# Layer 0 of a four-layer graph network: block sums made by accumulating transfers, the second half of x loaded early, its statistics on ScalarE

## The chip, the cores and the metric

The kernel runs on one core of one Trainium2 chip. The metric is the device time of one execution in microseconds; before the change the median of three executions is 2145.6 us (2143.03 to 2153.62). Five engines work side by side, each through its own list of instructions in order: TensorE (PE, with its weight loads PEld), VectorE (DVE), ScalarE (ACT), GpSimd (POOL) and SyncE (SP). SP and POOL issue the transfers, each through a queue of its own (q1 is SP's, q0 is POOL's), and 16 DMA engines carry them out. An instruction that waits holds back all that stand behind it on its engine.

## The reference, cut to what matters

x has 2708 rows and 512 columns, adj is 2708 by 2708, all in f32. Four layers follow each other; all have the product of a scaled adjacency matrix with a normalized x, and layer 0 is

```python
h = jnp.maximum(_layernorm(x, axis=-1), 0.0)
deg = jnp.sum(adj, axis=1)
dinv = (deg + 1.0) ** (-0.5)
aug = dinv[:, None] * (adj + jnp.eye(n)) * dinv[None, :]
x = x + jax.nn.relu(aug @ h @ weight)
```

## The kernel before

**Tiling.** The rows of x stand as 22 tiles of 128 rows by 512: 20 full ones (`NF`), five to each of four quarters, and two that hold what is left of the quarters (`NF`, `NF + 1`). The transposed adjacency stands in HBM as blocks `yb[j, i, u]` of 128 x 5 x 339 numbers (847.5 KB; j and i are quarters, u one of two halves of the 677 columns), and rows for the two odd tiles (`yt`).

**The products.** adj times h is done with Winograd's seven products on two levels. The outer seven, called p1 to p7 here, are in `OUTER`: p1 takes `XA` (tiles 0 to 9, first 256 columns) and y11 as it is, p2 `XC` and y21, p3 `XC` and y22, p4 `XD` and t4, p5 `XB` and t1, p6 `XA` and t2, p7 `XA` and t3. XB has the second 256 columns of tiles 0 to 9, XC and XD those of tiles 10 to 19. Their sums are t1 = y12 + y11, t3 = y22 + y12, t2 = y22 + t1 = t3 + y11 and t4 = t2 + y21, each of 2 x 2 blocks (`QUAD`, written (0,0), (0,1), (1,0), (1,1)) and two halves u; `keep_o` stores them through POOL's queue for the later layers (`osum`). `add_loops` puts the identity of aug into diagonal blocks. X itself is rewritten in place between the products (`by_halves`: XA - XB before p7; XA = -XD - XA before p6).

One `multiply` is one outer product for one u. It makes seven inner products of five matmuls each (L475; the trace counts each f32 matmul twice, so x10), in the order 1, 6, 2, 7, 5, 4, 3. `inner_x` (L436 to L439) forms s1 to s4 of the X side, `inner_y` (L449 to L452) forms t1, t2, t4 and t3 of the four blocks o11, o12, o21, o22. ACT copies product 1 into v (L503), DVE makes u2 and u3 (L507, L513), and `give` (L492, L494, L487) brings the results into `agg`. Product 6 needs inner t2, product 7 inner t3, product 4 inner t4.

**The order of layer 0** (`first_aggregate`). All first loads are for the degrees: PE adds up the blocks' columns (L275), `quarter_columns` and `first_h` turn the sums into dinv and write relu of the normalized x with it into h (L221). So h's first half is ready after the blocks of two quarters. Then follow, with u = 0 and 1 each, p1 and p7; beside p7 the degrees of the other half (`other_degrees`), and after it `first_h` for tiles 10 to 21; then p6, p2, p4 for u = 1, the same for u = 0; the odd tiles' products of quarters 0 and 1 (`tails`, L526, L531, L566); p5 for u = 0 and 1; the other tails, `epilogue`, p3, `epilogue`.

**Sums in layer 0.** `third_sums` (L644) forms t3 on DVE from y22 in its place and y12 in a spare block; `second_sums` (L651) adds t3 to y11 for t2, for both u; `first_stats` (L202, L203) takes mean and variance of x's second half on DVE, after its load (L238, L240) behind p7's first half. `first_sums` forms t1 by a load of y12 (L402) and a transfer that adds y11 to what lies in SBUF (`accum_op`, L697, issued by POOL), block by block; `add_loops` on its diagonal blocks (L410) and the stores follow one product later. Three spare blocks lie in the second half of h (`spare`), three in `agg` (`early`), three in `ends` (`more`).

**What sets the order.** The instructions are put in each engine's list when the program is built, by a scheduler. `tc.issue_after(i)` holds what is under it until after instruction i; the lists `at_u2`, `at_u3`, `at_end` and `at_t4` collect such instructions. Nothing reorders the lists on the chip. Transfers of SP use eight semaphores in turn, so that each waits for the landing of the one eight places before it.

Of the kernel before, what the change touches and what calls it, by code (L numbers as in the profile page):

```python
# [12 lines left out]
P = 128  # L13
# [24 lines left out]
def gnn_kernel(  # L38
# [178 lines left out]
        )  # L217
        return b

    def normalized(t, src, scale, shift):  # L220
        nc.scalar.activation(h[:, t, :], src, AF.Relu, bias=shift, scale=scale)  # L221

    def groups(ts):

# [17 lines left out]
    def first_stats(ts):  # L242
        for t in ts:
            stats(h[:, t, :], mv0[:, t, :])

# [68 lines left out]
    def other_degrees(u, ys):  # L314

        if u == 0:
            parts[1, 1] = upool.tile([P, W], FP, tag="s", name="row")
        for b, blocks in ((0, (ys[1], ys[2])), (1, (ys[7],))):
            ps = ps_out.tile([P, W], FP, tag="out", name="dg_ps")
            tl = tail_place(b, u)  # L320
            column_sums(ps, [tl[:, 0], tl[:, 1]], blocks, parts[b, u])
        if u < U - 1:
            return
# [15 lines left out]
    def first_h(columns, looped):  # L339

        ts = list(columns)
        n, t0 = len(ts), ts[0]
        span = slice(t0, t0 + n)
        pd = ps_sm.tile([P, NT], FP, tag="sm", name="pd")
        for s, t in enumerate(ts):
            nc.tensor.matmul(
                pd[:, s : s + 1], columns[t], ones[:, 0:1], start=True, stop=True
            )
        if looped:
            nc.vector.tensor_copy(deg[:, t0 : t0 + looped], pd[:, :looped])  # L350
        if looped < n:
            nc.vector.tensor_scalar(
                deg[:, t0 + looped : t0 + n], pd[:, looped:n], 1.0, None, ALU.add
            )
        rsqrt(dinv[:, span], deg[:, span], n)
        mv = mv0[:, span, :]
        rstd = rstd_of(mv, n)
        nc.vector.tensor_mul(rstd[:, :n], rstd[:, :n], dinv[:, span])
        sh = shift_of(mv, rstd, n)
        for s, t in enumerate(ts):  # L360
            normalized(t, h[:, t, :], rstd[:, s : s + 1], sh[:, s : s + 1])

    def other_roots():

# [55 lines left out]
        nc.vector.scalar_tensor_tensor(o, a, -1.0, b, ALU.mult, ALU.subtract)  # L420

    at_u2, at_u3, at_end, at_t4 = [], [], [], []

    def inner_x(X):
        n = half // 2
# [14 lines left out]
    def inner_y(blks, u, loops, t3=None):  # L442
# [8 lines left out]
        at_t4.append(nc.vector.tensor_add(t4, o21, t2).ins)  # L451
        nc.vector.tensor_add(t3, o22, o12)  # L452
        return {1: o11, 2: o21, 3: o22, 4: t4, 5: t1, 6: t2, 7: t3}

# [9 lines left out]
            multiply(xs_, inner_y(blks, u, loops), u, dests)  # L464
            free.extend(blks)

    def multiply(xs_, ys, u, dests):


        cu = slice(u * W, (u + 1) * W)  # L470
# [12 lines left out]
        def give(a, b, ps, part, op):  # L483
# [5 lines left out]
            for fh, ih, how in dests:  # L489
                d = agg[:, fh, ih, a, b, cu]  # L490
                if part is not None:
                    at_end.append(nc.vector.tensor_tensor(d, ps, part, op).ins)  # L492
                elif how == "added":
                    nc.vector.tensor_add(d, d, ps)  # L494
                elif how == "less":
                    nc.vector.tensor_sub(d, ps, d)
# [6 lines left out]
        nc.scalar.copy(v, pa)  # L503
        pb = bank("pb")
        product(pb, 6, True)
        u2 = upool.tile([P, W], FP, tag="u2", name="u2", bufs=2)
        at_u2.append(nc.vector.tensor_add(u2, v, pb).ins)  # L507
        product(pa, 2, False)
        give(0, 0, pa, None, None)
        pc = bank("pc")  # L510
        product(pc, 7, True)
        u3 = upool.tile([P, W], FP, tag="u3", name="u3")
# [38 lines left out]
    def tails(self_loops, qs, loaded=None):  # L551

        for q in qs:
            blk, both = loaded[q] if loaded else tail_rows(self_loops, q)
            for u in range(U):
# [7 lines left out]
                tail_products(ps, tl, True)  # L563
                for c in range(NC):
                    d = agg[:, c // 2, q // 2, c % 2, q % 2, u * W : (u + 1) * W]
                    nc.vector.tensor_add(d, d, ps[c])  # L566
            free.append(blk)

    H1 = list(range(0, half))
# [36 lines left out]
    def first_aggregate(epilogue):  # L606
# [25 lines left out]
        t3 = {0: [free.pop(0), free.pop(0), take(early), take(early)], 1: blks[0]}  # L632
        temps = spare + [take(early)]
        p1, p7 = (0, 0, "as it is"), (1, 1, "as it is")
        for u in range(U):
            for b in range(2):
                load_rows(*(tail_place(b, u)[:, s] for s in range(2)), yt[:, :, 2 + b, u])
        xs_ = inner_x(XA)
        multiply(xs_, ys, 0, [p1])
        ys = inner_y(blks[1], 1, 0, own_t3)  # L640

        def third_sums(u):
            for (a, b), blk, y in zip(QUAD, t3[u], temps):
                nc.vector.tensor_add(blk, blk, y)  # L644
                if a == b:
                    add_loops(blk, u, OUTER[7][2])
                keep_o(blk, "t3", a, b, u)

        def second_sums(u):
            for (a, b), t2, y in zip(QUAD, blks[u], t3[u]):  # L650
                nc.vector.tensor_add(t2, t2, y)  # L651
                keep_o(t2, "t2", a, b, u)

        for (a, b), blk, y in zip(QUAD, t3[0], temps):
            load_plain("y22", a, b, 0, blk)
            load_plain("y12", a, b, 0, y)
        with tc.issue_after(at_u2[-1]):
            third_sums(0)
        for (a, b), y in zip(QUAD, temps):
            load_plain("y12", a, b, 1, y)  # L660
        multiply(xs_, ys, 1, [p1])
        second_sums(0)
        by_halves(nc.vector.tensor_sub, XA, XA, XB)
        xs_ = inner_x(XA)
        ys = inner_y(t3[0], 0, 0, own_t3)
        last_sum = at_t4[-1]
        other_degrees(0, ys)
        for (a, b), blk in zip(QUAD, t3[1]):
            load_plain("y22", a, b, 1, blk)
        multiply(xs_, ys, 0, [p7])  # L670
        with tc.issue_after(last_sum):
            third_sums(1)
        first_x(range(half, NT))
        ys = inner_y(t3[1], 1, 0, own_t3)
        with tc.issue_after(at_u3[-1]):
            second_sums(1)
        with tc.issue_after(at_end[-1]):
            first_stats(range(half, NT))
        other_degrees(1, ys)
        multiply(xs_, ys, 1, [p7])  # L680
        first_part_of_both()
        by_halves(minus_sum, XA, XD, XA)
        free += t3[0][:2] + t3[1]

        def among(places):

            for k, f in enumerate(free):
# [1 line left out]
                    return free.pop(k)  # L689
            return free.pop(0)  # L690


        def first_sums(u, places):
            t1 = [among(places) for _ in QUAD]
            for (a, b), blk in zip(QUAD, t1):
                load_plain("y12", a, b, u, blk)
                nc.gpsimd.dma_start(blk, yb[a, b, u], accum_op=ALU.add)  # L697
            with tc.issue_after(at_u3[-1]):
                for (a, b), blk in zip(QUAD, t1):
                    if a == b:  # L700
                        add_loops(blk, u, OUTER[5][2])
                    keep_o(blk, "t1", a, b, u)
            return t1

        for u in reversed(range(U)):
            if u == 1:
                t2 = blks[1]
            else:
                t2 = [among(in_obuf) for _ in QUAD]
                for (a, b), blk in zip(QUAD, t2):  # L710
                    nc.sync.dma_start(blk, osum["t2", a, b, u])
            xs_ = inner_x(XA)
            multiply(xs_, inner_y(t2, u, 0, own_t3), u, [(0, 1, "added")])
            if u == 1:
                other_roots()
                nc.vector.tensor_sub(XB, XB, XD)
            y21 = [among(more) for _ in QUAD]
# [4 lines left out]
            for (a, b), t4, y in zip(QUAD, t2, y21):  # L722
                nc.vector.tensor_add(t4, t4, y)
                keep_o(t4, "t4", a, b, u)
            free += y21
            if u == 0:
                rows = [tail_rows(True, q) for q in (0, 1)]
            xs_ = inner_x(XD)
            multiply(xs_, inner_y(t2, u, 0, own_t3), u, [(1, 0, "as it is")])
            if u == 0:  # L730
                t1 = first_sums(0, more)
            free += t2
# [5 lines left out]
        multiply(xs_, inner_y(t1, 0, 0), 0, p5)  # L738
        free = [f for f in free if all(f is not e for e in more)]
        first = [f for f in t1 if all(f is not e for e in more)]  # L740
        t1 = first_sums(1, in_obuf)
        multiply(xs_, inner_y(t1, 1, 0), 1, p5)
        free += first + t1
        tails(True, (2, 3))
        epilogue(H1)
# [392 lines left out]
```

## Time and profile before

| What | Value |
|---|---|
| Runs, median (lowest to highest) | 2145.6 us (2143.03 to 2153.62) |
| The profiled execution's own time | 2147.35 us |
| Its span | 2145.6 us |
| PE busy | 2068.6 us, 96% |
| DVE busy | 1438.6 us, 67% |
| ACT busy | 384.7 us, 18% |
| Mean traffic | 167 GB/s |

The profile has one row for each instruction with its start, its length, what it writes and reads, and, where the engine was idle before it, how long and what ended the wait. A matmul's end is modelled. Times are counted from the start of the span. Layer 0's products fill the stretch from 35 us to about 449 us; the change touches what runs before 375 us.

### The profile page before, as it was taken

What the parts mean: (1) busy time and instruction counts of PE and PEld (TensorE: products, weight loads), DVE (VectorE), ACT (ScalarE), POOL (GpSimd) and SP (SyncE); (2) the same over time, 40 slices, a digit from 0 to 9 for tenths busy, and PEclk for the clock granted to TensorE, in tenths of its full rate; (3) what the DMA queues carried; (4) which work ended last, traced back from release to release, by engine and by line L of the source; (5) the groups of instructions that cost most, each with busy time, mean ns of one, the idle gap of its engine ahead of it and who ended that gap; (6) DMA issues with size and microseconds to landing.
All of it is one profiled execution on the core that took longest, in us unless ns stands there. A gap on an engine that the chain in (4) does not pass through costs nothing.

```text
span 2145.6 us, 19944 instructions
## 1 busy us (share of the span) xinstructions
PE 2068.6 (96%) x7310; PEld 1289.0 (60%) x7310; DVE 1438.6 (67%) x2513; ACT 384.7 (18%) x755; POOL 173.7 (8%) x319
## 2 busy tenths in 40 slices
PE   5989979999999999999999999999999999999998
PEld 2555646556666645566664546666677666666664
DVE  3888847667666867777576879968537755666512
ACT  1111000222000010100001121000116534444401
POOL 0000010211000020200001130000001000000001
PEclk9999989999999999999999999999999999999999
DMA  9884695446454443644453656544541233233212
GB/s 351 346 336 154 191 281 189 161 153 211 164 177 167 148 165 137 234 164 156 162 183 123 218 196 211 176 156 156 192 166 72 96 101 103 91 101 100 80 41 64
DMA packets 78720, 358.05 MB, mean 167 GB/s; under 512 B 10540, under 2 KB 14508, under 8 KB 78624
## 3 DMA queue, kind: packets, MB, share of 16 engines
q1 hardware_dynamic: 51104, 250.98, 34.3%
q0 software_dynamic: 27520, 105.82, 14.6%
q8 instruction: 57, 0.93, 0.2%
q14 instruction: 39, 0.32, 0.0%
HBM read 294.61 MB, written 62.15 MB: 166 GB/s over the span
## 4 chain that ended last, share of the span: by engine, by line
PE 62%; issue 20%; DMA 8%; DVE 7%; POOL 2%; ACT 1%; SPq 0%; POOLq 0%; DVEq 0%; ACTq 0%
PE pa L475 13%; PE pc L475 12%; PE pd L475 12%; PE po L754 7%; PE pb L475 6%; PE pe L1045 4%; PE pt L526 3%; PE pg L893 3%; DMA obuf<-in_yb_dram 2%; DMA h<-in_x_dram 1%; PE pt L531 1%; DVE ends L846 1%; POOL ends L761 1%; DMA ends<-xs 1%; DMA osumt<-obuf 1%
## 5 line engine op out<-in xcount | busy, mean ns | idle before, releaser
L1045 PE MATMUL pe<-obuf,h 128*128 128x339 f32 x1280 | 372.9, 448 | 0.0
L475 PE MATMUL pa<-obuf,h 128*128 128x339 f32 x1050 | 324.0, 454 | 13.4 <-DVE h L420 8.5
L1045 PEld LDWEIGHTS pe<-obuf,h 128*128 128x128 f32 x1280 | 241.2, 189 | 126.4 <-issue 10.0
L754 PE MATMUL po<-ends,agg 128*128 128x512 f32 x640 | 281.4, 596 | 2.1 <-ACT ends L774 1.9
L475 PEld LDWEIGHTS pa<-obuf,h 128*128 128x128 f32 x1050 | 200.1, 192 | 121.4 <-issue 9.4
L754 PEld LDWEIGHTS po<-ends,agg 128*128 128x128 f32 x640 | 119.8, 190 | 144.8 <-issue 137.3
L475 PE MATMUL pd<-obuf,s 128*128 128x339 f32 x550 | 169.0, 454 | 13.3 <-DVE agg L492 13.3
L475 PE MATMUL pc<-t,h 128*128 128x339 f32 x560 | 173.8, 457 | 4.4 <-DVE u L513 4.4
L966 ACT ACTIVATE e<-r,nsr 128x339 f32<-128x339 f32 x352 | 170.7, 566 | 28.6 <-DVE obuf L970 11.7
L475 PE MATMUL pb<-t,s 128*128 128x339 f32 x560 | 169.3, 448 | 0.1
L475 PE MATMUL pd<-t,s 128*128 128x339 f32 x560 | 169.2, 448 | 0.0
L503 ACT COPY v<-pa 128x339 f32<-128x339 f32 x56 | 24.6, 440 | 758.4 <-PE pa L475 738.8
L475 PEld LDWEIGHTS pd<-obuf,s 128*128 128x128 f32 x550 | 105.6, 192 | 68.0 <-DVE agg L492 14.3
L475 PEld LDWEIGHTS pc<-t,h 128*128 128x128 f32 x560 | 108.1, 194 | 60.9 <-DVE u L513 6.0
L475 PEld LDWEIGHTS pd<-t,s 128*128 128x128 f32 x560 | 106.0, 189 | 54.2 <-issue 0.5
L475 PEld LDWEIGHTS pb<-t,s 128*128 128x128 f32 x560 | 105.7, 189 | 54.6 <-DVE s L420 0.7
L475 PE MATMUL pc<-obuf,s 128*128 128x339 f32 x450 | 136.1, 448 | 0.0
L475 PEld LDWEIGHTS pc<-obuf,s 128*128 128x128 f32 x450 | 85.3, 189 | 43.6 <-issue 0.5
L450 DVE TENSOR_TENSOR t<-obuf,t 128x1695 f32<-128x1695 f32 x55 | 105.4, 1917 | 0.0
L780 POOL DMA_DIRECT2D xs<-ends x66 | 35.9, 544 | 817.6 <-DVE ends L779 764.8
L451 DVE TENSOR_TENSOR t<-obuf,t 128x1695 f32<-128x1695 f32 x53 | 101.6, 1917 | 0.0
L449 DVE TENSOR_TENSOR t<-obuf 128x1695 f32<-128x1695 f32 x49 | 94.1, 1920 | 9.8 <-DMA obuf<-in_yb_dram 6.6
(247 smaller groups left out, 2184.2 us busy)
## 6 DMA issues: line engine op xcount, KB each, us to landing
obuf<-in_yb_dram SPq DMA_DIRECT2D x131, 847.5 KB, 4.6
obuf<-osumt SPq DMA_DIRECT2D x100, 847.5 KB, 4.5
osumt<-obuf POOLq DMA_DIRECT2D x23, 847.5 KB, 9.0
xs<-ends POOLq DMA_DIRECT2D x66, 256.0 KB, 2.3
ends<-xs POOLq DMA_DIRECT2D x66, 256.0 KB, 3.4
obuf<-in_yt_dram SPq DMA_DIRECT2D x32, 339.0 KB, 3.6
h<-in_yb_dram SPq DMA_DIRECT2D x11, 847.5 KB, 10.0
ends<-in_yb_dram SPq DMA_DIRECT2D x11, 847.5 KB, 6.2
```

Source lines behind the costliest of these rows:

```text
L449: nc.vector.tensor_add(t1, o12, o11)
L450: nc.vector.tensor_add(t2, o22, t1)
L451: at_t4.append(nc.vector.tensor_add(t4, o21, t2).ins)
L475: nc.tensor.matmul(ps, xs_[q][:, k, :], ys[q][:, k, :], start=start and k == 0, stop=k == KT - 1, skip_group_check=not start,)
L503: nc.scalar.copy(v, pa)
L526: nc.tensor.matmul(ps[c], h[:, NF, c * P : (c + 1) * P], tl[:, 0, :], start=start, stop=False)
L531: nc.tensor.matmul(ps[c], h[g, NF + 1, c * P : (c + 1) * P], tl[g, 1, :], start=False, stop=True)
L754: nc.tensor.matmul(po, cs[c], w_sb[:, c, :], start=(c == 0), stop=(c == NC - 1))
L780: nc.gpsimd.dma_start(xs[t], xt)
L893: nc.tensor.matmul(pk, cs[c], wg_sb[:, c, k, :], start=(c == 0), stop=(c == NC - 1))
L966: nc.scalar.activation(e[:, k], row, AF.Exp, bias=nsr[:, t, s : s + 1], scale=1.0)
L1045: nc.tensor.matmul(pe[c], h[:, t, c * P : (c + 1) * P], a, start=(t == 0), stop=False)
```

## The change

- `accumulated` loads a block by SP (a plain part of y, or t3 from `osum`) and then adds a part of y to it by a POOL transfer. All four blocks of a sum are issued in one go, before the stores. t3 is made so for both u (y22, then y12), and t2 of u = 0 (t3 from `osum`, then y11); t1 goes on being made so. t2 of u = 1 stays a DVE sum, now just before p7's second half.
- The identity is added inside `inner_y` at the use. `inner_y` of p7, of p6 with u = 0, and of p5 is held by `issue_after` until near the end of the multiply before it; the stores of the sums stand behind the accumulating transfers.
- x's second half is loaded before p1. Its mean is taken on ACT (`other_stats`: Identity with accumulation over 512 columns) after p1's last v, the variance (Square with bias) after p7's first v.
- `first_h` writes h by halves of 256 columns, for tiles 10 to 21 the second half first; its chain is now called inside p7's second multiply, after u2. The copy of agg's first part to its second goes from ACT (L574) to a transfer of SP inside SBUF.
- The degrees' loads rotate among four places instead of six, since two of `early` now receive t3.

```diff
-    def normalized(t, src, scale, shift):
-        nc.scalar.activation(h[:, t, :], src, AF.Relu, bias=shift, scale=scale)
+    def normalized(t, src, scale, shift, fs=slice(0, D)):
+        nc.scalar.activation(h[:, t, fs], src[:, fs], AF.Relu, bias=shift, scale=scale)
...
+    def other_stats(ts, squares):
+        y = ytp.tile([P, 2, W], FP, tag="yt", name="y").rearrange("p s w -> p (s w)")[:, 0:D]
+        for t in ts:
+            if squares:
+                nc.scalar.activation(
+                    y, h[:, t, :], AF.Square,
+                    bias=mv0[:, t, 0:1], scale=-1.0, accum_out=mv0[:, t, 1:2],
+                )
+            else:
+                nc.scalar.activation(y, h[:, t, :], AF.Identity, accum_out=mv0[:, t, 0:1])
+        m = mv0[:, ts.start : ts.stop, int(squares)]
+        nc.scalar.activation(m, m, AF.Copy, scale=1.0 / D)
...
-        for s, t in enumerate(ts):
-            normalized(t, h[:, t, :], rstd[:, s : s + 1], sh[:, s : s + 1])
+        fs = slice(0, D // 2), slice(D // 2, D)
+        for f in fs if t0 < half else fs[::-1]:
+            for s, t in enumerate(ts):
+                normalized(t, h[:, t, :], rstd[:, s : s + 1], sh[:, s : s + 1], f)
...
+        if beside is not None:
+            with tc.issue_after(at_u2[-1]):
+                beside()
...
-        places = spare + early
+        t3 = {0: early[:2]}
+        places = spare + early[2:]
...
+        def accumulated(blks, key, u, source):
+            for (a, b), blk in blks.items():
+                if key in PLAIN:
+                    load_plain(key, a, b, u, blk)
+                else:
+                    nc.sync.dma_start(blk, osum[key, a, b, u])
+                j, i = PLAIN[source]
+                last = nc.gpsimd.dma_start(blk, yb[j + a, i + b, u], accum_op=ALU.add)
+            return last.ins
...
+        t3 = {0: [free.pop(0), free.pop(0)] + t3[0], 1: blks[0]}
+        came[0] = accumulated(dict(zip(QUAD, t3[0])), "y22", 0, "y12")
...
+        first_x(range(half, NT))
         xs_ = inner_x(XA)
         multiply(xs_, ys, 0, [p1])
         ys = inner_y(blks[1], 1, 0, own_t3)
+        came[1] = accumulated(dict(zip(QUAD, t3[1])), "y22", 1, "y12")
         multiply(xs_, ys, 1, [p1])
+        with tc.issue_after(at_v[-1]):
+            other_stats(range(half, NT), False)
         by_halves(nc.vector.tensor_sub, XA, XA, XB)
         xs_ = inner_x(XA)
+        for u in range(U):
+            with tc.issue_after(at_end[-2]):
+                ys = inner_y(t3[u], u, OUTER[7][2], own_t3)
+            with tc.issue_after(came[1]):
+                keep_all(t3[u], "t3", u)
+            other_degrees(u, ys)
+            if u == 0:
+                multiply(xs_, ys, u, [p7])
+                with tc.issue_after(at_v[-1]):
+                    other_stats(range(half, NT), True)
+        with tc.issue_after(at_end[-1]):
+            for t2, y in zip(blks[1], t3[1]):
+                nc.vector.tensor_add(t2, t2, y)
+        keep_all(blks[1], "t2", 1)
+        multiply(xs_, ys, 1, [p7], other_h)
+        nc.sync.dma_start(agg[:, 0, 1], agg[:, 0, 0])
         by_halves(minus_sum, XA, XD, XA)
...
+        def second_sums(a_b):
+            more_of_it = {ab: among(in_obuf) for ab in a_b}
+            t2[0].update(more_of_it)
+            return accumulated(more_of_it, "t3", 0, "y11")
...
+            if u == 1:
+                second_sums(QUAD[:2] + QUAD[3:])
...
             if u == 0:
-                t1 = first_sums(0, more)
+                t1 = [among(more) for _ in QUAD]
+                came = accumulated(dict(zip(QUAD, t1)), "y12", 0, "y11")
...
+        for u in range(U):
+            with tc.issue_after(came):
+                keep_all(t1, "t1", u, QUAD[1:3])
+            with tc.issue_after(at_end[-3]):
+                ys = inner_y(t1, u, OUTER[5][2], own_t3 if u == 0 else None)
+            with tc.issue_after(came):
+                keep_all(t1, "t1", u, QUAD[::3])
+            multiply(xs_, ys, u, p5)
+            if u == 0:
+                t1 = [free.pop(0) for _ in QUAD]
+                came = accumulated(dict(zip(QUAD, t1)), "y12", 1, "y11")
```

More of the change, by code (lines that the diff above doesn't have):

```diff
@@ L321, in other_degrees, with other_h @@
             column_sums(ps, [tl[:, 0], tl[:, 1]], blocks, parts[b, u])
-        if u < U - 1:
-            return
+    def other_h():
         columns = {}
@@ L420, in minus_sum @@
         nc.vector.scalar_tensor_tensor(o, a, -1.0, b, ALU.mult, ALU.subtract)
-    at_u2, at_u3, at_end, at_t4 = [], [], [], []
+    at_v, at_u2, at_u3, at_end = [], [], [], []
     def inner_x(X):
@@ L450, in inner_y @@
         nc.vector.tensor_add(t2, o22, t1)
-        at_t4.append(nc.vector.tensor_add(t4, o21, t2).ins)
+        nc.vector.tensor_add(t4, o21, t2)
         nc.vector.tensor_add(t3, o22, o12)
@@ L465, in outer_product, with multiply @@
             free.extend(blks)
-    def multiply(xs_, ys, u, dests):
+    def multiply(xs_, ys, u, dests, beside=None):
         cu = slice(u * W, (u + 1) * W)
@@ L493, in give @@
                 elif how == "added":
-                    nc.vector.tensor_add(d, d, ps)
+                    at_end.append(nc.vector.tensor_add(d, d, ps).ins)
                 elif how == "less":
-                    nc.vector.tensor_sub(d, ps, d)
+                    at_end.append(nc.vector.tensor_sub(d, ps, d).ins)
                 else:
@@ L502, in multiply @@
         v = upool.tile([P, W], FP, tag="v", name="v")
-        nc.scalar.copy(v, pa)
+        at_v.append(nc.scalar.copy(v, pa).ins)
         pb = bank("pb")
@@ L565, in tails @@
                     d = agg[:, c // 2, q // 2, c % 2, q % 2, u * W : (u + 1) * W]
-                    nc.vector.tensor_add(d, d, ps[c])
+                    at_end.append(nc.vector.tensor_add(d, d, ps[c]).ins)
             free.append(blk)
@@ L629, in first_aggregate @@
         blks = {u: [y11[a, b, u] for a, b in QUAD] for u in range(U)}
[L632 to L683, printed above, removed]
         def among(places):
@@ L690, in among @@
             return free.pop(0)
[L693 to L703, printed above, removed]
+        def accumulated(blks, key, u, source):
[7 more added lines that the diff above has]
+            return last.ins
@@ new lines, in keep_all @@
+        def keep_all(blks, key, u, a_b=QUAD):
+            for a, b in a_b:
+                keep_o(blks[QUAD.index((a, b))], key, a, b, u)
+        t3 = {0: [free.pop(0), free.pop(0)] + t3[0], 1: blks[0]}
+        came = {}
+        p1, p7 = (0, 0, "as it is"), (1, 1, "as it is")
+        came[0] = accumulated(dict(zip(QUAD, t3[0])), "y22", 0, "y12")
+        for u in range(U):
+            for b in range(2):
+                load_rows(*(tail_place(b, u)[:, s] for s in range(2)), yt[:, :, 2 + b, u])
@@ new lines, in first_aggregate @@
+        first_x(range(half, NT))
+        xs_ = inner_x(XA)
+        multiply(xs_, ys, 0, [p1])
+        ys = inner_y(blks[1], 1, 0, own_t3)
+        came[1] = accumulated(dict(zip(QUAD, t3[1])), "y22", 1, "y12")
+        multiply(xs_, ys, 1, [p1])
+        with tc.issue_after(at_v[-1]):
+            other_stats(range(half, NT), False)
+        by_halves(nc.vector.tensor_sub, XA, XA, XB)
+        xs_ = inner_x(XA)
+        for u in range(U):
[8 more added lines that the diff above has]
+                    other_stats(range(half, NT), True)
@@ new lines, in first_aggregate @@
+        with tc.issue_after(at_end[-1]):
[4 more added lines that the diff above has]
+        nc.sync.dma_start(agg[:, 0, 1], agg[:, 0, 0])
+        by_halves(minus_sum, XA, XD, XA)
+        free += t3[0][:2] + t3[1] + early[2:]
+        t2 = {1: dict(zip(QUAD, blks[1])), 0: {}}
+        def second_sums(a_b):
+            more_of_it = {ab: among(in_obuf) for ab in a_b}
+            t2[0].update(more_of_it)
+            return accumulated(more_of_it, "t3", 0, "y11")
@@ L705, in first_aggregate @@
         for u in reversed(range(U)):
+            t2u = [t2[u][ab] for ab in QUAD]
+            xs_ = inner_x(XA)
             if u == 1:
-                t2 = blks[1]
+                ys = inner_y(t2u, u, 0, own_t3)
             else:
[L709 to L713, printed above, removed]
+                with tc.issue_after(at_end[-2]):
+                    ys = inner_y(t2u, u, OUTER[6][2] - OUTER[7][2], own_t3)
+                with tc.issue_after(came):
+                    keep_all(t2u, "t2", u)
@@ L714, in first_aggregate @@
+            multiply(xs_, ys, u, [(0, 1, "added")])
+            u3_of_6 = at_u3[-1]
             if u == 1:
@@ L716, in first_aggregate @@
                 nc.vector.tensor_sub(XB, XB, XD)
-            y21 = [among(more) for _ in QUAD]
+            y21 = [among(more + early[2:]) for _ in QUAD]
             for (a, b), blk in zip(QUAD, y21):
                 load_plain("y21", a, b, u, blk)
+            if u == 1:
+                second_sums(QUAD[:2] + QUAD[3:])
             xs_ = inner_x(XC)
             multiply(xs_, inner_y(y21, u, 0, own_t3), u, [(0, 0, "added")])
[L722 to L726, printed above, removed]
+            with tc.issue_after(u3_of_6):
+                for t4, y in zip(t2u, y21):
+                    nc.vector.tensor_add(t4, t4, y)
+            keep_all(t2u, "t4", u)
+            free += [f for f in y21 if f is not early[2]]
+            if u == 1:
+                came = second_sums(QUAD[2:3])
+            else:
                 rows = [tail_rows(True, q) for q in (0, 1)]
             xs_ = inner_x(XD)
-            multiply(xs_, inner_y(t2, u, 0, own_t3), u, [(1, 0, "as it is")])
+            multiply(xs_, inner_y(t2u, u, 0, own_t3), u, [(1, 0, "as it is")])
             if u == 0:
-                t1 = first_sums(0, more)
-            free += t2
+                t1 = [among(more) for _ in QUAD]
+                came = accumulated(dict(zip(QUAD, t1)), "y12", 0, "y11")
+            free += t2u
         nc.vector.tensor_add(XC, XC, XA)
@@ L737, in first_aggregate @@
         p5 = [(0, 1, "less"), (1, 1, "less")]
-        multiply(xs_, inner_y(t1, 0, 0), 0, p5)
         free = [f for f in free if all(f is not e for e in more)]
         first = [f for f in t1 if all(f is not e for e in more)]
-        t1 = first_sums(1, in_obuf)
-        multiply(xs_, inner_y(t1, 1, 0), 1, p5)
+        for u in range(U):
+            with tc.issue_after(came):
+                keep_all(t1, "t1", u, QUAD[1:3])
+            with tc.issue_after(at_end[-3]):
+                ys = inner_y(t1, u, OUTER[5][2], own_t3 if u == 0 else None)
+            with tc.issue_after(came):
+                keep_all(t1, "t1", u, QUAD[::3])
[3 more added lines that the diff above has]
+                came = accumulated(dict(zip(QUAD, t1)), "y12", 1, "y11")
         free += first + t1
```

## The prediction, made before the changed kernel had run

> **What bounds the kernel now.** I read the page first. PE is busy 96% of the span, so a gain must come out of PE's idle or slow stretches; in the slices the granted clock dips below 9 only around 270 to 320 us.
>
> ```profile
> PE 2068.6 (96%) x7310; PEld 1289.0 (60%) x7310; DVE 1438.6 (67%) x2513; ACT 384.7 (18%) x755; POOL 173.7 (8%) x319
> PEclk9999989999999999999999999999999999999999
> DMA  9884695446454443644453656544541233233212
> ```
>
> Then PE's timeline, where brackets give the idle time before a row and what ended it:
>
> ```profile
> 116.70 3.12 PE L475 MATMUL pc<-t,h 128*128 128x339 f32 x10 [1.63 <-DVE u L513]
> ...
> 144.62 0.38 PE L346 MATMUL pd<-ones,across 128*128 128x1 f32 x2 [1.78 <-DVE across L286]
> ...
> 164.75 5.69 PE L475 MATMUL pa<-obuf,h 128*128 128x339 f32 x10 [8.53 <-DVE h L420]
> ...
> 297.77 5.74 PE L475 MATMUL pd<-obuf,s 128*128 128x339 f32 x10 [12.26 <-DVE agg L492]
> ...
> 316.43 2.35 PE L526 MATMUL pt<-obuf,h 128*128 128x339 f32 x4 [2.00 <-DVE agg L566]
> ```
>
> An inner product takes 3.02 us (2.86 from one to the next), and 5.7 after the two long gaps. From 57 us, where p1 sets in, to 375 us, idle time and slow products come to about 39 us. That is all there is to win. DVE ends each gap, and its timeline tells why:
>
> ```profile
> 83.35 3.75 DVE L651 TENSOR_TENSOR obuf<-obuf,ends 128x1695 f32<-128x1695 f32 x2
> ...
> 109.83 1.93 DVE L644 TENSOR_TENSOR obuf<-obuf,h 128x1695 f32<-128x1695 f32 x1 [3.60 <-DMA obuf<-in_yb_dram]
> ...
> 134.84 1.28 DVE L202 BATCH_NORM_STATS2 st<-h 128x6 f32<-128x512 f32 x2
> ...
> 294.07 0.65 DVE L410 SCALAR_TENSOR_TENSOR obuf<-ident,obuf 128x128 f32<-128x128 f32 x3 [13.17 <-DMA obuf<-in_yb_dram]
> ...
> 314.92 0.19 DVE L548 TENSOR_TENSOR obuf<-obuf,ident 128x32 f32<-128x32 f32 x1 [3.31 <-DMA obuf<-in_yt_dram]
> ```
>
> From 65 to 160 us DVE hardly rests, with a stall on data in between; at 281 it stands 13.17 us before an accumulated block of t1, and p4's last add and so PE stand behind it. Last, the accumulating transfers (L697) and what waits for them:
>
> ```profile
>   DVE obuf L410: 13.2, 1
> ...
> DMA to landing us min/median/max: 7.5/10.8/17.3
> ```
>
> **What is removed on DVE.** Eight L644 adds of 1.92 us (15.4), four of the eight L651 (7.7), twelve statistics of 0.64 and 0.09 (8.7): 32 us out of the stretch 65 to 145. The step times below are positions in the changed lists, with durations of these rows; long adds follow each other every 1.84 us.
>
> **Until p1.** The degrees' blocks landed every 2.1 us until 50 us, and PE waited for them. With four places, quarter 1's first load stands behind the reading of quarter 0's (PE, by 22 us); the transfers ahead of it land until 29.6, so the queue does not run dry: 0 (bounds 0 to +2, one block). The half normalization may bring p1's second product forward; it already ran at low clock (4.81 for 10): 0 (to -2).
>
> **p7, first half.** inner_y now stands behind p1's last but one give, at 94.0. Behind that: by_halves 1.4, three s of 0.74, a give 0.42, loops 1.2, t1, t3, t2 of 1.84 each: t2 at 104.7, where before it was there at 101. Product 6 starts at 104.8 instead of 102.6; in return the 1.63 goes and PE has the third sum's dg matmuls already behind it: p7's first half ends at 120.3 instead of 122.6: -2.3. It costs +4 more if one more 1.84 add and the loops fall behind.
>
> **p7, second half, and the chain to p6.** DVE from 118.0: loops 1.0, t1, give, t2, t3, t4 to 127.1, four t2 adds to 134.4, u2, ten small copies to 135.6. PE meanwhile: column sums, products 1, 6, 2, 7 to 135.1, so the copies arrive just as it reaches its small matmuls (12 of 0.23). Products 5, 4, 3 end at 146.1 (before 156.2). The chain deg, roots, scale takes 8.6 us, as DVE still puts t2, t4 and t3 of p6 between its steps; ACT starts at 150.1 (before 159.54). Five halves, then L420 with 1.49: PE at 153.9 instead of 164.75. So far -10.9. The idle time before p6 stays 7.8, and with it the slow product. A 256-wide activation is not in the trace: between 0.44 (L503, 339 wide) and 0.73 (3.63 for five of 512); five make 2.2 to 3.6. I take 0.44, so +1.4 at most. The later 0.53 before product 2 (v behind twelve rows of ACT) goes: -11.5.
>
> **Statistics on ACT.** 24 passes over 512 columns are not in the trace; nearest is L221 with 0.71, so 17 us, on an engine with 3.2 us of work from 60 to 120. They are hidden by p1 and p7; v and the PSUM copy stand behind them. The first twelve must be done when p7's first product ends (102), since its v and a copy of column sums stand behind them: x must land by 92 at 0.71 us a pass, by 84 at 1.4, twice that. A gain is excluded, since v waits for PE alone today. I take the nearest row and 0; both mishaps together (x at 92, passes of 1.4) cost +8.
>
> **Accumulating transfers.** They take DVE's place on the path: DVE's loops and adds of p7 wait for them, and the gives behind those. The trace's packet records give 0.26 us for a plain packet of 6780 bytes and 0.53 for an accumulating one; a block is 8 of them on each engine, 2.1 and 4.2 us. Where both queues had work, they took turns packet by packet, 6.3 us a pair. t3's loads for u = 0 land from 52 to 65, its four additions by 75 (due 95.6); x (2 KB packets, 0.1 us) until 84; y22 for u = 1 behind it; its additions at 6.3 or less until 112, due 118.6. The slack is about 7 us; t2's last block lands near 212, due 219. Eight stores, which used to go out from 77, now follow: DMA is idle from 150 on (share 0.22 to 0.25). The copy inside SBUF has no row like it: 1356 KB, at the plain rate 3.4 us, by the median landing of blocks into h (10.0 for 847.5 KB) 16. It waits on SP for p7's first half and its stores (near 121) and holds up one block of y21 and the reloads of t3 behind it, which are due after 160; its own reader adds at 165: 0. The y21 loads ahead of it wait for stores that now follow the additions (near 118, due 160): 0.
>
> The Trainium skill (SBUF — State Buffer, "SBUF: two separate sides") speaks against this: POOL must write a transfer's descriptors and can be locked out by some VectorE work, and an example there went from 0.62 to 3.1 us. In the trace an accumulating issue took 0.91 us at 247.9 beside a busy DVE and 0.90 each at 279.5 beside a waiting one, so the lock is not seen. By the rule the last addition could come 2.5 us later, still inside the slack: 0 in either case.
>
> **p6, p2, p4.** PE runs without a gap before (170 to 285) and DVE's list there loses nothing it needs: 0. Then p4's last product has no wait on t1 in front: 12.26 and 2.72 of slow clock: -26.5.
>
> **Tails and p5: given back.** The loads for tails 2 and 3 still need blocks that tails 0 and 1 free, so DVE still waits at L548: of the 3.8 us over the bare 13.0 that the four groups take, 1.3 stay (-29.0). But p5's inner_y, done before the tails so far, now stands behind the third last tail add, with L578 (2.98), loops 0.8, three adds of 1.84: t2 at 300.5 while PE is there at 297.9, after a wait of 1.3 for the loops. With 0.9 of tail matmuls drawn forward: +4.5. p5's second half waits about 0.5; the tails after it are 1.5 shorter: -25.5. DVE's old stall of 2.0 at the tails was followed by four matmuls in 2.35 us instead of 1.41, the 1.63 one by none slower, so the clock may cost up to +1 here.
>
> The Trainium skill (TensorE: Matmul & The Clock Gate, "What's actually happening") counts only idle windows of about 3.4 us; by it those 2.6 us would cost no clock. The 2.00 us row contradicts it, and I keep the row's +1 as a bound.
>
> The sum is made against the profiled span, 2145.6 us, the same number as the median of the runs: 2145.6 - 25.5 = **2120 us**. Its own range: all bounds of gain (-2, p7's t2 in time -2.2, p5's in time -4) 2112; of loss (+2, +4, +1.4, +1) 2128.
>
> **Rivals.**
> - *Additions for u = 1 late, moderately* (15%). For it: 90 to 140 is full today (share 1.02), and the median landing is 10.8. If eight land one by one from 53 at 10 each, the last comes at 133: p7's second half 14 late: 2134. Against: 279.5 and 280.1 were issued together and landed about 4 us apart.
> - *Slower* (12%): the same place, at 14.4 each, as the addition at 258 took beside loads and stores. The last lands at 168, 50 late; p4's and the tails' gains (14) stay: 2120 + 50 = 2170. It is slower than before from 11.4 us a block on (118.6 + 25.5 - 53, over 8). Against: those 14.4 held a store, two loads and an addition.
> - *The t1 wait stays* (10%): t1 was accumulated before, and DVE can stand at p5's loops just as at L410. Additions are no longer held behind stores in POOL's list, and p4's loads come 12 us earlier with it; the fourth should land by 265, due 290. If it came 13 late of that, 15 of the gain go: 2135. ACT's copies late by 8 would end alike, 2128.
>
> **The numbers.** Forecast 63%, rivals 15, 12, 10. The range 2111 to 2138 takes in the two middle cases. A measurement here tells 0.5% (10.7 us) from no change: faster 0.75 (forecast and most of the first rival), same 0.12, slower 0.13.
>
> **What would show it.** Right: no L644 rows, p7's halves ending near 120 and 146; the wait before p6 still near 8 us, at 154; no 12.26 before p4's last product; a new wait of 1 to 3 us at p5's product 6. Wrong: DVE's L410 successor waiting for a DMA before p7 or p5, ACT's v late behind the statistics, or PE waiting longer for the degrees before 57 us.

## The result, and the profile after

| | Median of the runs | Lowest to highest | Against before, 95% interval |
|---|---|---|---|
| before, 22 runs | 2144.18 us | 2140.42 to 2153.62 | |
| after, 22 runs | 2149.22 us | 2145.47 to 2153.54 | 1.0021 [1.0013, 1.0029] |

The forecast was 2120 us. The change made the kernel 0.2% slower: the interval is clear of 1, but the step is smaller than the 0.5% that the prediction set as the least that can be told, and the time lies above the range of 2111 to 2138. The two profiled executions hide even that: the one of before took 2147.35 us, 3 above its median, the one of after 2146.61, 3 below its own, so their spans differ by only -0.8 us.

The page of after has a first line and three groups that answer to what was shown of before (out<-in, count, busy and mean, then idle time ahead of the group and what ended most of it):

```profile
PE 2066.2 (96%) x7310; PEld 1284.2 (60%) x7310; DVE 1409.6 (66%) x2483; ACT 406.8 (19%) x826; POOL 184.1 (9%) x331
...
L492 PE MATMUL pa<-obuf,h 128*128 128x339 f32 x1040 | 320.5, 453 | 12.8 <-DVE h L438 7.7
...
L492 PE MATMUL pc<-t,h 128*128 128x339 f32 x560 | 171.5, 452 | 7.1 <-DVE u L533 7.1
...
L492 PE MATMUL pd<-obuf,s 128*128 128x339 f32 x550 | 166.3, 448 | 1.5 <-DVE agg L509 1.5
```

VectorE does 29 us less, as the prediction had it (32), and the 12.26 us ahead of p4's last product are gone (that group's idle time was 13.3). Yet PE's idle time, span less busy, is 78.6 us against 77.0: products 7 wait 7.1 us in all (4.4 before), and layer 0's tails wait 12.2 (2.6 before). PE's timeline says where:

```profile
156.30 4.58 PE L492 MATMUL pa<-obuf,h 128*128 128x339 f32 x10 [7.71 <-DVE h L438]
...
217.31 4.79 PE L492 MATMUL pc<-t,h 128*128 128x339 f32 x10 [3.33 <-DVE u L533]
...
224.79 3.02 PE L492 MATMUL pa<-obuf,h 128*128 128x339 f32 x10
...
282.72 3.02 PE L492 MATMUL pd<-obuf,s 128*128 128x339 f32 x10
...
306.20 2.63 PE L546 MATMUL pt<-obuf,h 128*128 128x339 f32 x4 [10.11 <-DVE agg L586]
311.14 3.17 PE L492 MATMUL pa<-ends,h 128*128 128x339 f32 x10 [1.21 <-DVE ends L428]
...
321.29 3.12 PE L492 MATMUL pb<-t,s 128*128 128x339 f32 x10 [1.03 <-DVE t L467]
```

p4's last product (282.72) follows without a gap. Two long waits are new: 3.33 us and a slow product inside p4's first multiply (u = 1), and 10.11 us inside the tails of quarters 0 and 1. VectorE's timeline shows what it stood at when PE waited for its u3 and its tail adds:

```profile
210.42 0.20 DVE L568 TENSOR_TENSOR obuf<-obuf,ident 128x32 f32<-128x32 f32 x1 [4.39 <-DMA obuf<-in_yt_dram]
216.64 0.16 DVE L568 TENSOR_TENSOR obuf<-obuf,again_ident 128x5 f32<-128x5 f32 x1 [6.03 <-DMA obuf<-in_yt_dram]
...
302.69 0.20 DVE L568 TENSOR_TENSOR obuf<-obuf,ident 128x32 f32<-128x32 f32 x1 [9.42 <-DMA obuf<-in_yt_dram]
305.56 0.16 DVE L568 TENSOR_TENSOR obuf<-obuf,again_ident 128x5 f32<-128x5 f32 x1 [2.67 <-DMA obuf<-in_yt_dram]
```

These are identity adds of at most 0.2 us to the odd tiles' rows (L548 before). Nobody needs the first two before the tails at 285 us, or the last two before 357. But they stand early in VectorE's list, ahead of the u3 and the tail adds that PE waits for, and their rows came later than VectorE. The DMA view of the stretch 255 to 320 us (issues: count, size of each, median us to landing) has them, for before and for after:

```profile
obuf<-in_yb_dram POOLq DMA_DIRECT2D x5, 847.5 KB, 10.4
...
obuf<-in_yt_dram SPq DMA_DIRECT2D x3, 339.0 KB, 5.8
```

```profile
obuf<-in_yb_dram POOLq DMA_DIRECT2D x5, 847.5 KB, 20.6
...
obuf<-in_yt_dram SPq DMA_DIRECT2D x4, 339.0 KB, 11.7
```

The same small loads took 11.7 us instead of 5.8 (medians), beside accumulating transfers that took 20.6 us from issue to landing instead of 10.4.

Set beside the prediction's sum, by the starts of PE's work in the two profiles (after less before):

| Place | Predicted | Measured |
|---|---|---|
| p6 begins | -10.9 | -8.45 |
| p4's first multiply begins | -11.5 | -8.7 |
| p6, u = 0 (p4's first multiply over) | -11.5 | -3.4 |
| tails 0 and 1 begin (p4 over) | -26.5 | -17.8 |
| p5 begins | -29.0 | -9.0 |
| p5, u = 1 | -24.5 | -4.6 |
| projection after the tails | -25.5 | -2.5 |

### The profile page after: what moved, and what is told of

Same layout as the page of the kernel before. It is cut to its first block, busy times and chain, and to the rows that moved or that the text cites. A ratio compares the mean times of both kernels' runs of the same rounds, so it can differ in the third digit from the quotient of the medians.

```text
span 2144.8 us, 20020 instructions
## 1 busy us (share of the span) xinstructions
PE 2066.2 (96%) x7310; PEld 1284.2 (60%) x7310; DVE 1409.6 (66%) x2483; ACT 406.8 (19%) x826; POOL 184.1 (9%) x331
## 3 DMA queue, kind: packets, MB, share of 16 engines
q0 software_dynamic: 29248, 116.24, 16.6%
## 4 chain that ended last, share of the span: by engine, by line
issue 43%; PE 42%; DMA 7%; DVE 5%; POOL 3%; ACT 0%; POOLq 0%; SPq 0%; ACTq 0%; DVEq 0%
PE pa L492 9%; PE pc L492 9%; PE pd L492 9%; PE po L785 5%; PE pb L492 5%; DMA obuf<-in_yb_dram 2%; PE pt L546 2%; DMA ends<-xs 1%; PE pg L924 1%; POOL ends L792 1%; DMA xs<-ends 1%; DVE ends L877 1%; PE pt L551 1%; POOL xs L811 1%; POOL out_dram L1028 1%
## 5 line engine op out<-in xcount | busy, mean ns | idle before, releaser
L997 ACT ACTIVATE e<-r,nsr 128x339 f32<-128x339 f32 x352 | 170.6, 566 | 28.0 <-DVE obuf L1001 11.7
L466 DVE TENSOR_TENSOR t<-obuf 128x1695 f32<-128x1695 f32 x49 | 94.0, 1918 | 12.5 <-DMA obuf<-in_yb_dram 6.8
## 6 DMA issues: line engine op xcount, KB each, us to landing
obuf<-in_yb_dram SPq DMA_DIRECT2D x130, 847.5 KB, 4.5
obuf<-osumt SPq DMA_DIRECT2D x100, 847.5 KB, 4.5
osumt<-obuf POOLq DMA_DIRECT2D x23, 847.5 KB, 10.6
obuf<-in_yb_dram POOLq DMA_DIRECT2D x13, 847.5 KB, 15.7
ends<-in_yb_dram SPq DMA_DIRECT2D x11, 847.5 KB, 9.3
```

The lines of the kernel that those rows point to most:

```text
L997: nc.scalar.activation(e[:, k], row, AF.Exp, bias=nsr[:, t, s : s + 1], scale=1.0)
```

## The experiments

Each ratio is against the kernel before on the same chip. The theory after the result: the savings are real, and the row adds, late because the accumulating transfers fill the queues, give them back.

**1. The changed kernel again.**

> The changed kernel once more, unaltered, so that the others can be set beside it on the same chip, and to see how far its waits differ from one profiled execution to the next. All theories: 1.001 to 1.003 of the time before. Theory (late rows): VectorE again stands at the identity adds of the odd tiles' rows in p4's first multiply (some 10 us) and inside the tails of quarters 0 and 1 (some 8 us).

2148.16 us, 1.0024 [1.0014, 1.0034]. PE waited 4.10 us at p4's first multiply and 10.15 in the tails; p5 began at 313.03. The waits belong to the kernel, not to one execution.

**2. Row adds late.**

```diff
-                rows = [tail_rows(True, q) for q in (0, 1)]
+                rows = [tail_rows(False, q) for q in (0, 1)]
...
+        with tc.issue_after(at_u2[-1]):
+            for q in (0, 1):
+                tail_loops(rows[q][1], q)
         tails(True, (0, 1), rows)
...
-        tails(True, (2, 3))
+        tails(True, (2, 3), None, at_u2[-1])
```

> The identity adds of the odd tiles' rows are held on VectorE until the u2 of the multiply ahead of their use; loads and traffic as they were. Theory (late rows): 9 to 14 us less than the changed kernel. p6's second multiply begins near 219 instead of 224.8, and the wait of 10 us inside the tails of quarters 0 and 1 is gone, p5 beginning near 299 instead of 311. Rival A (t1 sets the end): t1's last blocks land at 295 and 320 anyway, so p5 waits for them, and no more than 4 us come out. Rival B (the traffic slows all alike, the adds are only where it is seen): within 2 us of the changed kernel.

2144.0 us, 1.0006 [0.9997, 1.0015]: 4.2 less than run 1, where the theory said 9 to 14. Both waits did go, and p5 began at 296.76 instead of 313.03. Then PE's and VectorE's timelines show a wait that was not there before:

```profile
348.11 5.67 PE L492 MATMUL pc<-t,h 128*128 128x339 f32 x10 [11.58 <-DVE u L533]
```

```profile
334.12 0.65 DVE L428 SCALAR_TENSOR_TENSOR obuf<-ident,obuf 128x128 f32<-128x128 f32 x3 [2.15 <-DMA obuf<-in_yb_dram]
345.72 1.93 DVE L466 TENSOR_TENSOR t<-obuf 128x1695 f32<-128x1695 f32 x1 [10.95 <-DMA obuf<-in_yb_dram]
```

VectorE now stands at the loops and the first inner sum of p3, two steps ahead of their use, for y22 blocks that land at 334.10 and 345.62; p5's u3 is behind them. The theory's number missed, since it stopped at the first wait; rival A's "no more than 4" is nearly met, but by y22 and not by t1.

**3. t1's additions left out** (t1 is y12 alone).

```diff
         def accumulated(blks, key, u, source):
+            if source == "y11" and key in PLAIN:
+                for (a, b), blk in blks.items():
+                    load_plain(key, a, b, u, blk)
+                return at_u2[-1]
```

> t1's eight accumulating transfers are left out, so t1 is y12 alone; all else as changed. Theory (late rows, and their lateness comes from the accumulating transfers, 34 us of queue time between 257 and 320): the rows loaded at 290 land within 5 us instead of 12 to 14, and the 10 us inside the tails of quarters 0 and 1 go; the 5 us at p4's first multiply stay, as t2's additions lie there: 8 to 11 us less than the changed kernel. Rival A (t1 sets the end): the same 8 to 11 or more, since t1 is there early. Rival B (VectorE itself is too full in the tails): within 3 us.

2133.67 us, 0.9959 [0.9945, 0.9972]: 14.5 less than run 1. The rows landed 3.0 and 3.5 us after their issue, and the 10 us went, while p4's first multiply still waited 3.64 us, as expected. The slow matmuls behind the 10 us went too (2.63 us for four in run 1, 1.41 without a wait), which the expected 8 to 11 had left out; where another 2 us come from the profiles don't show. VectorE's list is the same, so rival B falls. Rival A expected as much; run 2 speaks against it, where t1 was as late as ever and p5 began 16 us earlier.

**4. t4's sums not held**, so that t1 begins earlier.

```diff
-            with tc.issue_after(u3_of_6):
-                for t4, y in zip(t2u, y21):
+            for t4, y in zip(t2u, y21):
```

> The t4 sums are no longer held behind p6's u3, as in the kernel before; t1's loads, which need the blocks that these sums read, should go out near 243 instead of 250. Theory (late rows): the queue empties earlier by some 7 us, so the rows loaded at 290 find less ahead of them: 2 to 6 us less than the changed kernel. Rival A (t1 sets the end): 5 to 7 us less. Rival B (the row adds alone, whatever the queue): 0 to 1.

2147.69 us, 1.0023 [1.0014, 1.0032]: as run 1, a miss. t1's additions began at 246.66 instead of 259.49 and the last landed at 309.30 instead of 321.65, but the rows, loaded at 289.42 and 290.31, still landed at 300.68 and 305.73, with POOL's additions landing beside them until 309.30.

**5. Row adds late, and p3's VectorE work behind the tails** (run 2's edit and this one).

```diff
+        last = at_end[-1]
         epilogue(H1)
-        outer_product(3, True, (0, 1, "added"))
+        with tc.issue_after(last):
+            outer_product(3, True, (0, 1, "added"))
```

> As the run with the late row adds, and p3's VectorE work (its identity adds and inner sums, which wait for y22) held behind the last add of the tails. That run had shown a new wait of 11.6 us at p5's second multiply, behind these. Theory (VectorE, in order, stands at early work whose data the full queues bring late): both waits go, the projection begins near 355 us instead of 369, and the time falls to 2128 to 2133 us, 15 to 19 below the changed kernel's 2148. Rival A (a next wait of the same kind takes it up again, on t1 or on the weights): 2138 or more. Rival B (traffic slows all alike): 2143 or more.

2131.56 us, 0.9945 [0.993, 0.996], inside the theory's 2128 to 2133: 0.55% faster than the kernel before, 0.8% faster than the changed one. PE's timeline:

```profile
281.77 3.02 PE L492 MATMUL pd<-obuf,s 128*128 128x339 f32 x10
...
298.27 3.17 PE L492 MATMUL pa<-ends,h 128*128 128x339 f32 x10 [1.20 <-DVE ends L428]
...
308.42 3.12 PE L492 MATMUL pb<-t,s 128*128 128x339 f32 x10 [2.26 <-DVE t L467]
...
355.96 31.17 PE L797 MATMUL po<-ends,agg 128*128 128x512 f32 x72
```

Neither hold changes what is loaded: SP and POOL issue the same transfers in the same order as in the changed kernel. The projection begins at 355.96 instead of 371.58 because VectorE no longer stands at work that is not yet due.

**6. t1 and p5 as before**, the rest as changed (`first_sums` back, p5's inner sums ahead of the tails).

```diff
-                t1 = [among(more) for _ in QUAD]
-                came = accumulated(dict(zip(QUAD, t1)), "y12", 0, "y11")
+                t1 = first_sums(0, more)
...
+        multiply(xs_, inner_y(t1, 0, 0), 0, p5)
...
+        t1 = first_sums(1, in_obuf)
+        multiply(xs_, inner_y(t1, 1, 0), 1, p5)
```

> The changed kernel, with t1 and p5 as in the kernel before: loads and additions block by block, the identity adds and stores behind p4's u3, p5's inner sums ahead of the tails. Theory (t1's part gained some 15 and gave back about as much, at the rows and at p5): the wait of some 12 us ahead of p4's last product is back, the waits in the tails are under 5, and the time is 2145 to 2151 us, near the changed kernel's 2148. Rival C (t1's part is what costs; the first part's 8 us are there to keep): 2137 to 2142.

2155.79 us, 1.0058 [1.0044, 1.0073]: slower than either expectation. PE's timeline:

```profile
299.03 4.62 PE L492 MATMUL pd<-obuf,s 128*128 128x339 f32 x10 [16.82 <-DVE agg L509]
...
323.34 2.63 PE L546 MATMUL pt<-obuf,h 128*128 128x339 f32 x4 [9.33 <-DVE agg L586]
```

t1's fourth block landed at 295.31 (294.05 in the kernel before), so what the first part saves only lengthens the wait in front of it, 12.26 to 16.82; and the rows were late here too, asked for at 308.66 and 309.55 and there at 318.54 and 322.68. Rival C is out: t1's part saves 7 us (1.0058 less 1.0024) even with its two waits.

**7. As run 5, with t4's sums not held.**

> As the run with late row adds and late p3, and the t4 sums no longer held behind p6's u3, so that t1's first additions begin near 246 instead of 257. Theory: p5's product 6 still waits about 2 us for t1 in the run without this; that goes: 1 to 3 us less than that run. Rival A (the additions, each alone, go no faster, as the queue is full): within 1 us of it.

2134.61 us, 0.996 [0.9945, 0.9976]; run 5's interval overlaps. The 2 us did not come: PE waited 1.03 and 1.45 us in p5 where run 5 waited 2.26, and the product behind took 4.81 us instead of 3.12.

**8. The two holds of run 5 on the kernel before.**

> The kernel before, with the same two holds (row adds late, p3's VectorE work behind the tails). It tells how much of the gain of the two holds is due without the change. Theory: in the kernel before, t1's wait of 12 us ahead of p4's last product sets the pace, and the rows cost 2 to 3: 1 to 4 us less than the time before. Rival D (the holds are worth as much without the change, which then brings nothing): 12 us less or more.

2142.49 us, 1.0 [0.9989, 1.0011], where the theory said 1 to 4 us less. The profile has the old wait in its place:

```profile
295.51 5.68 PE L475 MATMUL pd<-obuf,s 128*128 128x339 f32 x10 [12.07 <-DVE agg L492]
```

So the holds alone are worth nothing that can be measured, the change alone +5 us, and both together -12 (0.9945 of 2144).

**9. p3's work late, alone** (run 5's edit without run 2's).

> The changed kernel with p3's VectorE work alone held behind the tails; the row adds stay where they were. The late row adds alone gave 4 us, both holds together 17. Theory (waits in series: what is late first hides what is late next): within 2 us of the changed kernel, 2146 to 2150, since VectorE stands only 1.7 us at p3's blocks there. Rival (p3's early work is the real cost, the row adds a side matter): 8 us less or more.

2146.79 us, 1.0016 [1.0006, 1.0025], as the theory had it. One hold gives 4.2, the other 1.7 (0.0008 of 2144, with run 1's interval overlapping), both 17 (1.0024 less 0.9945): waits in series.

**10. p5's inner sums earlier**, on run 5.

```diff
-        ends_of_sums()
+        nc.vector.tensor_add(agg[:, 1, 1], agg[:, 1, 1], agg[:, 0, 1])
...
-            with tc.issue_after(at_end[-3]):
+            with tc.issue_after(at_end[-5 if u == 0 else -3]):
                 ys = inner_y(t1, u, OUTER[5][2], own_t3 if u == 0 else None)
+            if u == 0:
+                with tc.issue_after(at_t2[-1]):
+                    nc.vector.tensor_add(agg[:, 1, 0], agg[:, 1, 0], agg[:, 1, 1])
```

> As the run with both holds, and p5's first inner sums drawn forward ahead of the last four adds of the tails and of the 3 us sum of agg's parts, which now follows them. In that run p5's product 6 began at 308.4, 11.4 us after the tails' last matmul. Theory: t1's fourth block lands at 294, so product 6 can begin near 303; p5's second half then waits about 2 us for t1's last block (319): 2 to 5 us less than that run's 2131.6. Rival A (t1's second half sets the end): within 1 us of it.

2132.43 us, 0.994 [0.9927, 0.9952]: no gain over run 5 that can be told. VectorE and PE:

```profile
295.72 0.65 DVE L428 SCALAR_TENSOR_TENSOR obuf<-ident,obuf 128x128 f32<-128x128 f32 x3 [3.82 <-DMA obuf<-in_yb_dram]
```

```profile
301.76 5.18 PE L492 MATMUL pb<-t,s 128*128 128x339 f32 x10 [5.88 <-DVE t L467]
```

Product 6 began at 301.76, but after a wait of 5.88 it ran slow, and p5's second half began 264.9 us after p1's second product, where run 5 had 262.9. Rival A's number is met, though by another block: t1's fourth of u = 0 landed at 295.70 and VectorE waited 3.82 us for it.

**11. t1's additions as plain copies** of the same blocks (t1 is y11 alone).

```diff
+                if source == "y11" and key in PLAIN:
+                    last = nc.gpsimd.dma_start(blk, yb[j + a, i + b, u])
+                else:
```

> The changed kernel with t1's eight accumulating transfers issued as plain ones of the same blocks (t1 is then y11 alone). Theory (an accumulating transfer takes the queues twice as long): 17 us of queue time less between 257 and 320; the rows loaded near 290 land in 5 to 8 us; 6 to 11 us less than the changed kernel, 2137 to 2142. Rival (their number and bytes count, not their rate): within 3 us of it, 2145 or more.

2142.87 us, 0.9994 [0.9985, 1.0003]: 6.4 us less than run 1 by the ratios, at the lower end of the theory. The DMA view of 255 to 320 us, first of run 1, then of this run:

```profile
DMA packets 3616, 20.13 MB, mean 310 GB/s; under 512 B 396, under 2 KB 396, under 8 KB 3614
...
obuf<-in_yt_dram SPq DMA_DIRECT2D x4, 339.0 KB, 11.7
```

```profile
DMA packets 4525, 24.36 MB, mean 375 GB/s; under 512 B 531, under 2 KB 531, under 8 KB 4523
...
obuf<-in_yt_dram SPq DMA_DIRECT2D x4, 339.0 KB, 5.6
```

The same issues in the same lists; a fifth more bytes pass in the stretch, and the rows come in half the time (medians). The two rows that the tails wait for, loaded at 291.68 and 292.57, took 6.88 and 8.93 us (12.00 and 13.95 in run 1), and PE's wait there fell by half, from 10.15 us to 5.13:

```profile
302.16 2.63 PE L546 MATMUL pt<-obuf,h 128*128 128x339 f32 x4 [5.13 <-DVE agg L586]
```

In run 3, without these transfers, it was gone. So about half of the lateness in the tails is the accumulating transfers' rate; the other half is that these eight transfers of 847.5 KB are in the queues there at all. VectorE's order makes PE pay for both.

**12. Statistics back on VectorE**, on run 5.

```diff
-        with tc.issue_after(at_v[-1]):
-            other_stats(range(half, NT), False)
...
-                with tc.issue_after(at_v[-1]):
-                    other_stats(range(half, NT), True)
+                with tc.issue_after(at_u2[-1]):
+                    first_stats(range(half, NT))
```

> As the run with both holds, and the statistics of x's second half back on VectorE, after the u2 of p7's first half (12 pairs, 8.8 us). Theory (in the changed kernel VectorE stands idle some 11 us between 105 and 119, so p7's first half is set by PE): within 1.5 us of the run with both holds, 2130 to 2133. Rival (as the prediction had it: these 8.7 us stand in the list that sets the end of p7): 5 to 9 us more.

2131.15 us, 0.9939 [0.9926, 0.9951]: as run 5. VectorE's timeline there, with the statistics between two of PE's hand-overs:

```profile
109.58 0.51 DVE L524 TENSOR_TENSOR u<-v,pb 128x339 f32<-128x339 f32 x1 [3.60 <-PE pb L492]
110.01 1.28 DVE L202 BATCH_NORM_STATS2 st<-h 128x6 f32<-128x512 f32 x2
...
119.33 0.48 DVE L509 TENSOR_TENSOR agg<-pc,u 128x339 f32<-128x339 f32 x1
```

They fill time in which VectorE waited for PE anyway. In run 5's kernel, with x loaded early, moving them to ScalarE bought nothing.

## Why the prediction was wrong

**The step that failed.** "p6, p2, p4. PE runs without a gap before (170 to 285) and DVE's list there loses nothing it needs: 0", and, of the tails, "1.3 stay (-29.0)". Each accumulating transfer was checked against the due time of its own block; what it does to others was not. The small loads that share the queues with them were left at the price of before. In place of 0, p4's first multiply lost 5.3 us (from -8.7 to -3.4 in the table); in place of 1.3 us over the bare 13.0, the tails of quarters 0 and 1 took 12.5, so that 8.8 us were lost there (from -17.8 to -9.0) where 2.5 should have been won. That makes 16.6 of the 23 us between the forecast and the two profiles; 2.8 are missing at p7 (below), 3.1 behind the start of p5's second half, whose waits the experiments don't take apart, and 0.7 at p4's last product.

Run 2 showed that both waits stand at the row adds, and run 5 that with them and the next ones of their kind gone 17 us come back. What makes the rows late is shown for the tails alone, by runs 3 and 11. At p4's first multiply those runs still waited 3.64 and 3.85 us, since t1's transfers come later. The trace of after has VectorE at the add from 206.0 us, before the rows were asked for (206.58 and 207.72); the first took 3.72 us, the second 8.82, beside t2's last addition (206.23 to 214.80) and a store. In the kernel before, the two were asked for before VectorE was there and took 2.97 and 3.62. That the addition and the store delay the second row is read from this, not tested.

That VectorE stands at L548 in the tails the prediction had seen, at the price of before; that an engine stands in order at work not yet due was no rival of it. Its own slower rival (t3's additions at 14.4 us each) was the wrong place: they landed at 111.60, as forecast. All its signs of being right came (no L644 rows, 7.71 us before p6, no wait before p4's last product, 1.03 at p5's product 6; p7's halves end at 121.8 and 148.4) and none of its signs of being wrong, since no sign looked at the row adds.

**A wrong date in it.** The prediction has "the fourth should land by 265, due 290"; t1's fourth block landed at 295.61. Two reasons lie in the trace: the loads went out at 250.15, since t4's sums (L743) ran from 248.17 and not from 230.34 as before; and the additions landed 6.2 us apart, as plain loads for p5's second half alternated with them. The wait in front of p4 still went, as its readers had been moved behind the tails.

**A mis-sized term: p7.** Predicted -10.9 at p6, measured -8.45 between the two profiles. p7's first half ended 0.8 us earlier instead of 2.3: t2 was there at 103.8, even before the 104.7 forecast, but PE had column sums and products to do without a pause and began product 6 at 106.27. From 95 to 148 us PE does not stop, so what VectorE saves beyond that is worth nothing, as run 12 shows for the statistics. The later v wait (-0.6) went, and a wait of 1.44 for an s came in its place. Against run 8's profile, counted from p1's second product, run 5 gains 4.3 at p6; so the term is 4 to 8 us. Two profiles of the same code differ by half of that: so counted, p6 begins at 107.4 us in the profile of before and at 105.0 in run 8's, whose code is the same up to there.

**Right.** p4's last product lost its wait and its slow product: 14.3 between the profiles, 15.0 forecast. p5's give-back: 4.4 measured (the table's steps at p5), 4.5 forecast, but the match is partly luck: 3.1 of it are tail matmuls drawn forward into p5 (0.9 forecast) and only 1.03 the wait at product 6; the wait for the loops, 1.21, came as forecast but falls into the tails' step. Statistics on ACT, hidden: 0. Additions of t3 for u = 1 by 112 (111.60), x by 84 (85.02). The copy inside SBUF took 13.5 us from 125.41 and nobody waited. The wait before p6 stayed near 8 (7.71). The chain from the degrees to ACT took 8.8 us (8.6).

**Together.** Run 5, with the waits at the row adds and at p3 out, is 12 us under the kernel before, not 25.5: against run 8 its profile has the front at -4.3 instead of -11.5, p4's wait at -14.0 instead of -15.0, p5 at +4.4 as forecast. Which waits lift the changed kernel's median 5 us above before's, when two profiles show -0.8, is not settled; over the twelve profiles with its front p1's second product began anywhere between 55.42 and 59.96 (57.31 and 57.97 with the old one), so single profiles differ by that much from the start on.

## What to carry to other kernels

When a change gives the DMA queues more to do, list every transfer that shares them in that stretch, not only the new ones, and see which engine stands in order at each landing; a 0.2 us add can stop everything behind it. A wait that is taken away uncovers the next one in the list, so single fixes look small until the last is in: test them together and, as a control, on the kernel before. Put work that waits for a load behind the last thing that is due before it, even if the schedule has room for it earlier.

## What the runs showed of the hardware

- In run 1 between 274 and 300 us an accumulating packet of 6780 bytes took 525 ns and a plain one beside it 272; in run 11 plain packets in both queues took about 260. The four additions for u = 0 landed 6.2 us apart in run 1, the copies in their place 2.8 to 5.0 in run 11. The Trainium skill (DMA: Bandwidth & Descriptors, "🎯 Rules for kernel authors") says that an accumulating transfer reads its destination and writes it later. That would fit twice the time; no run here separates the two.
- The same page ("Issuing engines are not separate DMA queues") says that transfers of all issuing engines share the same 16 engines and interleave. The rows, issued by SP, took 11.7 us beside POOL's accumulations and 5.6 beside POOL's copies: agreed, and it is the rule that the prediction should have applied to the rows.
- In the profile of after, an accumulating pass over 512 columns on ACT is two instructions, 0.63 us (Identity) or 0.72 (Square) and 0.19, and takes 0.76 or 0.85 from one pass to the next.
- After a wait a product is slow or not, and the length of that wait alone does not say which: after 2.31 us (run 2) it took 3.12, after 2.50 (run 12) 4.81, after 1.45 with 1.03 shortly before (run 7) 4.81. The granted clock goes with it: 1.00 from 300 to 310 us in run 2, 0.60 from 306.5 to 309.5 in run 12, 0.58 from 306.2 to 308.0 in run 7.
